# State sums two tiles at a time, and convolution taps loaded again for each image

## The chip, the cores and the metric

The kernel runs on one core of a Trainium2 chip. The metric is device time in microseconds (us), the median of several runs; lower is better. The core has five engines with a queue each: TensorE (PE) multiplies matrices into PSUM, VectorE (DVE) and GpSimd (POOL) work element by element, ScalarE (ACT) applies functions, and SyncE (SP) here issues nearly all DMAs. Each engine runs its own instructions in program order and waits on semaphores for the others.

## The reference, cut to what matters

The input `x` has four images of 128 channels and 64 x 64 pixels (L = 4096), in float32. Four layers follow, each of the form x + f(group_norm(x)):

```
x = x + attention(gn(x))        # one head over 4096 positions, 128 channels
x = x + conv5x5(gn(x))          # taps built from small tables by index
x = x + selective_scan(gn(x))   # 1x1 conv, two directions of 64 channels, 64 states each, 1x1 conv
x = x + conv3x3(gn(x))          # the offset branch of the reference does not change its result
```

The scan is the long part. For each channel and state it computes h[t] = exp(delta[t] * A) * h[t-1] + delta[t] * x[t] * B[t] over the 4096 positions, and then y[t] = sum over the 64 states of C[t] * h[t], plus D * x[t].

## The kernel before, in words

**The scan** (`scan_core`, L1159 to 1327) works in ticks. A tick is one tile of 128 partitions x 1024 positions: 32 channels of one direction with 4 states each. The loops run, outermost first, over image b, chunk c of 1024 positions, direction d, state group q (16 groups of 4 states), and channel group g (2 groups of 32): 256 ticks an image, 1024 in all. In each tick

- POOL makes the drive, `db = dx * br` (`drive`, L1227);
- ACT makes the decays, `da = exp(de * a)`, in two halves in PSUM, from three banks (`decay`, L1220);
- DVE scans them (`recur`, L1237) and multiplies the states by the row of C, into a tile `hc` (L1240); for two of five ticks or so POOL does this product instead (`weigh`, L1258);
- TensorE sums `hc` over states with a 128 x 32 matrix of ones, `sel`, into a PSUM bank `y` (`collect`, L1272). `collect` acts at every second tick, when both channel groups of a state group are there: 2 halves x 2 channel groups = 4 matmul instructions, each in 32 columns of the array, and each seen in the profile as two MATMULs. After the 16th state group a product with `skip` (L1283) closes the bank and ACT copies it out (`ys`, L1298).

The tiles `hc` come from a pool of 6. DMAs on SP's queue bring the operands four ticks ahead (`load`, L1188 to 1207): rows of B and C (`br`, `cr`, L1203) for each state group, `de` and `dx` (L1197) for each new chunk, direction and channel group.

**Everything else** is written as a generator, `images` (L1449), that yields an estimate of TensorE time after each few instructions. The loop at L1517 alternates between the scan's half ticks and this generator by a credit of 2.8 us a tick (`PACE`; 1.5 for the last image). So the instruction order on every engine is written out by this loop: while image b is scanned, attention, 5x5 convolution and operands of image b + 1 are woven between its ticks; the 3x3 convolutions of images 0 to 2 are woven into the scan of the last image, and the last one follows it (`conv_last`, L707).

**Attention** (`attention`, L434) takes score blocks of 128 x 512: a product `sc` (L479), an exponential on ACT into a ring of 8 slots (L485), and a product `acc` with the values (L491). The ring is the tile `exchange`, 128 x 4096, which later holds `delta` for the scan's operands. Every fourth block the sums of the exponentials are made on TensorE, in 32 columns as well (`sums`, L513). `sums_due` (L499) places them right after a `collect` where it can, by the mark "collected", and lets them wait three blocks at most.

**The 5x5 convolution** (`conv_pairs`, L810) treats output rows in pairs. Its matrices are the 25 taps and 10 sums of taps, all in one tile `cw` of 35 x 128 columns that stays in SBUF (L223). A chunk makes first `pq`, with the sums (`SUM12`, `SUM34`), and then two banks `pe`, with taps (L936). The first image uses four extra matrices in `more` and the pool `fill`, as nothing is scanned yet. The tables are built once on DVE (`build_conv_weights`, L231); 15 matrices are stored to DRAM in `kept` for a second program, which runs only if a sum of exponentials leaves its range. The first 15 places of `cw` serve the 3x3 convolution later.

Of the kernel before, what the change touches and what calls it, by code (L numbers as in the profile page):

```python
# [24 lines left out]
F32 = mybir.dt.float32  # L25
I32 = mybir.dt.int32
AF = mybir.ActivationFunctionType
ALU = mybir.AluOpType
# [4 lines left out]
P = 128  # L33
GROUPS = 32
GN_EPS = 1e-5
CH = 1024
# [16 lines left out]
def conv_preact_kernel(  # L53
# [166 lines left out]


    SUM12, SUM34, HSUM, HDIF = 5, 6, 7, 8
    cw = const.tile([P, NTAP + 10, C], F32, name="cw")  # L223
    taps5 = cw[:, :NTAP, :]

    m3 = cw[:, : main_w.shape[1], :]

    LSUM, LDIF, NKEPT = 9, 12, 15
    kept = dram.tile([P, NKEPT, C], F32, tag="kept", bufs=1, name="kept")

    def build_conv_weights(tmp):  # L231
        xx_sb = tmp.tile([P, NTAP, C], F32, name="xx_sb")
        nc.sync.dma_start(xx_sb, xhat)
        id_sb = tmp.tile([P, C], F32, name="id_sb")
        nc.sync.dma_start(id_sb, identity)
        picked = tmp.tile([P, 2, NTAP, C // 2], F32, name="picked")
        for n, (which, table, inds) in enumerate((("xx", wxx, indsxx), ("id", wid, indsid))):
            nr, oc = table.shape[1], table.shape[2]
            acc = picked[:, n]
            one = cw.rearrange("p k c -> p (k c)")[:, : NTAP * oc]  # L240
            one = one.rearrange("p (k o) -> p k o", o=oc)
            tab = tmp.tile([P, nr, oc], F32, name=f"tab{which}")
            nc.sync.dma_start(tab, table)
            ii = tmp.tile([P, NTAP], I32, name=f"ii{which}")
            nc.sync.dma_start(ii, inds.to_broadcast([P, NTAP]))
            fi = tmp.tile([P, NTAP], F32, name=f"fi{which}")
            nc.vector.tensor_copy(fi, ii)

            ng = tmp.tile([P, NTAP], F32, name=f"ng{which}")
            nc.vector.tensor_scalar(ng, fi, 0.0, float(nr), ALU.is_lt, ALU.mult)  # L250
            nc.vector.tensor_tensor(fi, fi, ng, ALU.add)
            nc.vector.tensor_scalar(fi, fi, 0.0, float(nr - 1), ALU.max, ALU.min)
            for r in range(nr):
                hit = tmp.tile([P, NTAP], F32, name=f"hit{which}{r}")
                nc.vector.tensor_scalar(hit, fi, float(r), None, ALU.is_equal)
                hit_b = hit.unsqueeze(2).to_broadcast([P, NTAP, oc])
                tab_b = tab[:, r : r + 1, :].to_broadcast([P, NTAP, oc])
                if r == 0:
                    nc.vector.tensor_tensor(acc, tab_b, hit_b, ALU.mult)
                else:  # L260
                    nc.vector.tensor_tensor(one, tab_b, hit_b, ALU.mult)
                    nc.vector.tensor_tensor(acc, acc, one, ALU.add)
                yield HOP

        for t in range(2):
            def every(ap):
                return ap.rearrange("p k (o t) -> p k o t", t=2)[:, :NTAP, :, t]

            idb = id_sb.rearrange("p (o t) -> p o t", t=2)[:, :, t].unsqueeze(1)
            idb = idb.to_broadcast([P, NTAP, C // 2])  # L270
            nc.vector.tensor_tensor(every(xx_sb), every(xx_sb), picked[:, 0], ALU.mult)
            nc.vector.tensor_tensor(every(cw), picked[:, 1], idb, ALU.mult)
            yield HOP
        nc.vector.tensor_tensor(taps5, taps5, xx_sb, ALU.add)
        for n in range(2):
            row = cw[:, (1 + 2 * n) * 5 :]
            nc.vector.tensor_tensor(
                cw[:, NTAP + n * 5 : NTAP + (n + 1) * 5, :], row[:, :5], row[:, 5:10], ALU.add
            )
        nc.sync.dma_start(kept, cw[:, :NKEPT, :])  # L280

# [150 lines left out]
    def attention(b, xs, xn, v, st, safe, loads):  # L434
# [188 lines left out]
        for w in (N - 2, N - 1) if fill else ():  # L623
            side_sums(w)
        blk = NM - 1
        values(N - 4)
        yield PRODUCT
        while due:
            sums(due.pop(0)[0])
            yield PRODUCT  # L630
        if not fill:
            sums(N - 1)
            yield PRODUCT
        evict_sums(blk)
        values(N - 3)
        yield PRODUCT
        turn(blk)
        values(N - 2)
        yield PRODUCT
        invert(blk)  # L640
        values(N - 1)
# [56 lines left out]


    def last_weights():  # L700
        half, above = cw[:, LSUM : LSUM + 3, :], cw[:, LDIF : LDIF + 3, :]
        nc.vector.tensor_tensor(half, m3[:, 0:3, :], m3[:, 6:9, :], ALU.add)
        nc.vector.tensor_scalar(half, half, 0.5, None, ALU.mult)
        nc.vector.scalar_tensor_tensor(above, m3[:, 3:6, :], -0.5, half, ALU.mult, ALU.add)
        nc.vector.scalar_tensor_tensor(half, m3[:, 3:6, :], 0.5, half, ALU.mult, ALU.add)

    def conv_last(b, xs, st, finish):  # L707
# [8 lines left out]
        def flat(t):  # L716
            return t.rearrange("p (h w) -> p h w", w=W)
# [30 lines left out]
        def products(acc, view, w):  # L748

            for n, dx in enumerate((1, 0, 2)):  # L750
                to = slice(max(1 - dx, 0), W - max(dx - 1, 0))
                of_ = slice(max(dx - 1, 0), W - max(1 - dx, 0))
                nc.tensor.matmul(  # L753
                    flat(acc)[:, :, to], cw[:, w + dx, :], view[:, :, of_],
                    start=n == 0, stop=n == 2, skip_group_check=True,
                )

# [36 lines left out]

    def more_weights(to):

        w = [cw[:, n * 5 : (n + 1) * 5, :] for n in range(3)]
        half, dif = to[:, 0], to[:, 1]  # L800
        nc.vector.tensor_tensor(half, w[0], w[2], ALU.add)
        yield HOP
        nc.vector.tensor_scalar(half, half, 0.5, None, ALU.mult)
        yield HOP
        nc.vector.scalar_tensor_tensor(dif, w[1], -0.5, half, ALU.mult, ALU.add)
        yield HOP
        nc.vector.scalar_tensor_tensor(half, w[1], 0.5, half, ALU.mult, ALU.add)
        yield HOP

    def conv_pairs(b, xs, tag, st, st2, lean):  # L810
# [87 lines left out]
        differences(0)  # L898
        K5 = 5
        steps, done = [], None  # L900

        def add(c, y, acc):
            i = 2 * c + y
# [6 lines left out]
        for c in range(L // CH):  # L910
# [20 lines left out]
            for n, (acc, parts) in enumerate(accs):  # L931
                k, total = 0, len(parts) * K5
                for w, view, r in parts:
                    for dx in range(K5):
                        k += 1
                        nc.tensor.matmul(  # L936
                            flat(acc), cw[:, w * K5 + dx, :] if w < HSUM else more[:, w - HSUM, dx, :],
                            view(r, dx), start=k == 1, stop=k == total and (n == 0 or not lean),
                        )
                        if k == 3 and done is not None:  # L940
                            done()
                            done = None
                        if k % 3 == 0:
                            yield 3 * PRODUCT
# [214 lines left out]
    def scan_core(mats4, ynds, before, widen, result):  # L1159
# [100 lines left out]
        def collect(i):  # L1260
# [2 lines left out]
            b, c, d, q, g = ticks[i]  # L1263
            if g + 1 < KG:
                return
            if q == 0:
                yacc[0] = bank("y", f"y_{b}_{c}_{d}")
            y = yacc[0]
            for h in range(CH // MM):
                for gg in range(KG):  # L1270
                    r = h * HALF + gg * SG
                    nc.tensor.matmul(  # L1272
                        y[r : r + SG, :], sel, hcs[i - KG + 1 + gg][:, bass.ts(h, MM)],
                        start=q == 0, stop=False, tile_position=(0, r), skip_group_check=True,
                    )
            ready.add("collected")
            for gg in range(KG):
                del hcs[i - KG + 1 + gg]
            if q + 1 < NQ:
                return  # L1280
            for h in range(CH // MM):
# [62 lines left out]
    def program(safe):  # L1344
# [2 lines left out]
        ready.clear()  # L1347
        shared.clear()
        if safe:
            nc.sync.dma_start(cw[:, :NKEPT, :], kept)  # L1350

        def load(tile, b):
            for c in range(NCH):
# [109 lines left out]
        with ExitStack() as es, tc.manual_schedule():  # L1463
# [19 lines left out]
            if not safe:  # L1483
                with tc.tile_pool(name="fill", bufs=2) as pools["fill"]:
                    while not (0, "begun") in ready:
                        next(work)
                    more = pools["fill"].tile([P, 2, 5, C], F32, tag="more", bufs=1, name="more")

                    with tc.tile_pool(name="tables", bufs=1) as tmp:
                        for _ in chain(scan_constants(), build_conv_weights(tmp), more_weights(more)):  # L1490
                            for _ in range(4):
                                next(work)
                    while (0, "convolved") not in ready:
                        next(work)
                del pools["fill"]
                setup.close()
            pools["rep"] = es.enter_context(tc.tile_pool(name=f"rep{safe}", bufs=3))
            pools["rows"] = es.enter_context(tc.tile_pool(name=f"rows{safe}", bufs=3))
            pools["hc"] = es.enter_context(tc.tile_pool(name=f"hc{safe}", bufs=6))
            pace = PACE  # L1500

            def before(b):
# [105 lines left out]
```

## Time and profile before

| | us |
|---|---|
| median of 3 runs | 4472.4 (4471.19 to 4475.15) |
| the profiled execution, its own time | 4469.3 |
| its span | 4467.5 |
| PE busy | 3980.8 (89%) |
| DVE busy | 3726.3 (83%) |
| POOL busy | 3638.1 (81%) |
| ACT busy | 2399.7 (54%) |
| `collect` on PE (L1272), 4096 MATMULs | 654.6 |
| DMA | 719.86 MB, 161 GB/s over the span |

A line of the profile names the source line, engine, operation, and output <- inputs by the program's tile names. "128*32" after a TensorE operation is the part of the array that it uses. Busy time of TensorE is modelled, as its instructions are pipelined: a MATMUL shows as about 0.6 us while the next one starts 0.43 us after it. PEld are weight loads. SPq is SP's queue of DMAs. The mean granted TensorE clock was 0.942 of full speed.

Stages by the span's time: image 0 without a scan to about 700 us; then attention, 5x5 convolution and operands of image 1 (738 to 1686), image 2 (1686 to 2633) and image 3 (2633 to 3540), each under the scan of the image before it; then the last scan to 4412, and the last 3x3 convolution to the end.

### The profile page before, as it was taken

To read this page: it belongs to the slowest core of one execution; us is meant where nothing else is said; L and a number is where in the kernel's file an instruction comes from. 1 tells how busy PE (TensorE), PEld (TensorE's weight loads), DVE (VectorE), ACT (ScalarE), POOL (GpSimd) and SP (SyncE) were. 2 spreads that over 40 slices of the span, in tenths; PEclk is the share of its full clock that TensorE was granted. 3 is DMA by queue.
4 is the path that set the end of the run, shared out by engine and by line. 5 is a ranking of instruction groups with operands and counts; after the bars stand their busy time and mean duration, and the time that the engine had idled before them with its cause. 6 is when DMAs were issued, how large, how long until landed. Compare 5 with 4: busy or idle time off the path is not lost. (4 is left out here: it accounts for less than half of the span.)

```text
span 4467.5 us, 43584 instructions
## 1 busy us (share of the span) xinstructions
PE 3980.8 (89%) x13480; PEld 1470.8 (33%) x13480; DVE 3726.3 (83%) x3703; ACT 2399.7 (54%) x4425; POOL 3638.1 (81%) x1728
## 2 busy tenths in 40 slices
PE   8999997999999979999999989999999758576776
PEld 4444433333333323333333333333333112121222
DVE  4712217999999989999999899999999899999995
ACT  3333217666665476666664576666654744444542
POOL 3433207999999978999999889999999889999995
PEclk9999999999999999999999999999999879787888
DMA  1000016544454565454545565455445666656562
GB/s 63 9 1 1 0 51 227 177 171 169 171 186 158 176 224 202 172 177 172 175 152 171 202 236 177 163 177 179 170 163 177 220 221 204 227 202 230 185 229 79
DMA packets 210002, 719.86 MB, mean 161 GB/s; under 512 B 24800, under 2 KB 25696, under 8 KB 209632
## 3 DMA queue, kind: packets, MB, share of 16 engines
q1 hardware_dynamic: 208160, 716.26, 45.9%
q8 instruction: 108, 1.77, 0.2%
q14 instruction: 134, 1.10, 0.1%
q10 hardware_dynamic: 1600, 0.73, 0.1%
HBM read 649.07 MB, written 67.83 MB: 160 GB/s over the span
## 5 line engine op out<-in xcount | busy, mean ns | idle before, releaser
L1227 POOL TENSOR_TENSOR db<-dx,br 128x1024 f32<-128x1024 f32 x1024 | 2399.9, 2365 | 231.1 <-DMA br<-bm 55.0
L1220 ACT ACTIVATE da<-de,a_neg 128x512 f32<-128x512 f32 (+1 forms) x1796 | 1342.9, 751 | 665.3 <-DVE da L1237 378.0
L479 PE MATMUL sc<-r,x 128*128 128x512 f32 x2048 | 1084.4, 612 | 16.0 <-ACT r L448 11.5
L491 PE MATMUL acc<-exchange,v 128*128 128x512 f32 x2048 | 1048.4, 594 | 1.7
L1258 POOL TENSOR_TENSOR hc<-hc,cr 128x1024 f32<-128x1024 f32 x401 | 947.7, 2363 | 19.3 <-ACT last L1253 16.5
L485 ACT ACTIVATE exchange<-sc 128x512 f32<-128x512 f32 x1024 | 604.7, 591 | 590.5 <-PE sc L479 583.8
L1272 PE MATMUL y<-hc,sel 128*32 128x512 f32 x4096 | 654.6, 652 | 270.6 <-POOL hc L1258 261.1
L1240 DVE TENSOR_TENSOR hc<-da,cr 128x512 f32<-128x512 f32 (+1 forms) x1078 | 835.5, 775 | 69.7 <-issue 0.9
L1237 DVE TENSOR_TENSOR_SCAN da<-da,last,db 128x512 f32<-128x512 f32 (+1 forms) x464 | 728.2, 1569 | 14.4 <-POOL db L1227 10.7
L1237 DVE TENSOR_TENSOR_SCAN da<-da,da,db 128x512 f32<-128x512 f32 x455 | 585.7, 1287 | 22.6 <-ACT da L1220 21.8
L479 PEld LDWEIGHTS sc<-r,x 128*128 128x128 f32 x2048 | 360.1, 190 | 607.8 <-issue 380.4
L491 PEld LDWEIGHTS acc<-exchange,v 128*128 128x128 f32 x2048 | 387.0, 190 | 496.7 <-issue 478.4
L1237 DVE TENSOR_TENSOR_SCAN hc<-da,last,db 128x512 f32<-128x512 f32 (+1 forms) x304 | 455.7, 1499 | 3.7 <-POOL db L1227 1.9
L1237 DVE TENSOR_TENSOR_SCAN hc<-da,hc,db 128x512 f32<-128x512 f32 x317 | 406.7, 1283 | 41.4 <-ACT da L1220 11.4
L533 POOL TENSOR_TENSOR sidep<-sidep,exchange 128x512 f32<-128x512 f32 x120 | 170.5, 1421 | 279.1 <-ACT exchange L485 276.9
L1272 PEld LDWEIGHTS y<-hc,sel 128*32 128x32 f32 x4096 | 92.9, 111 | 727.6 <-POOL hc L1258 350.9
L533 DVE TENSOR_TENSOR sided<-sided,exchange 128x512 f32<-128x512 f32 x120 | 96.1, 801 | 227.4 <-ACT exchange L485 226.1
L936 PE MATMUL pe<-df,cw 128*128 128x512 f32 x560 | 253.3, 597 | 0.0
L1237 DVE TENSOR_TENSOR_SCAN da<-da,db 128x512 f32<-128x512 f32 (+1 forms) x159 | 236.0, 1484 | 13.0 <-ACT da L1220 8.6
L678 PE MATMUL pcm<-xpm,cw 128*128 128x512 f32 x432 | 227.0, 670 | 15.5 <-ACT xpm L384 15.5
L513 PE MATMUL zp<-exchange,ones 128*32 128x512 f32 x1536 | 201.6, 596 | 8.0 <-DVE xs L580 7.9
L1253 ACT COPY last<-da 128x1 f32<-128x1 f32 x474 | 73.9, 156 | 249.4 <-DVE hc L1240 247.4
(239 smaller groups left out, 2829.8 us busy)
## 6 DMA issues: line engine op xcount, KB each, us to landing
br<-bm SPq DMA_DIRECT2D x512, 512.0 KB, 5.2
cr<-cm SPq DMA_DIRECT2D x512, 512.0 KB, 3.9
de<-dd SPq DMA_DIRECT2D x64, 512.0 KB, 4.7
dx<-dxd SPq DMA_DIRECT2D x64, 512.0 KB, 6.2
x<-in_x_dram SPq DMA_DIRECT2D x16, 512.0 KB, 5.1
xs<-in_x_dram SPq DMA_DIRECT2D x16, 512.0 KB, 5.6
xsd<-xs SPq DMA_DIRECT2D x16, 512.0 KB, 6.7
xcd<-xc SPq DMA_DIRECT2D x16, 512.0 KB, 2.8
```

What stands on the lines that cost most here:

```text
L479: nc.tensor.matmul(sc, xn[:, bass.ts(j, P)], rq[blk], start=True, stop=True)
L485: nc.scalar.activation(pt, sc, AF.Exp)
L491: nc.tensor.matmul(acc[blk], v[:, j, :], ring[:, u % NRING, :], start=j == 0, stop=j == NJT - 1)
L533: eng.tensor_tensor(s, s, ring[:, u % NRING, :], ALU.add)
L678: nc.tensor.matmul(acc.rearrange("p (r w) -> p r w", w=W), weights[:, t, :], xp[:, y : y + RPM, dx : dx + W], start=t == 0, stop=t == k * ...
L936: nc.tensor.matmul(flat(acc), cw[:, w * K5 + dx, :] if w < HSUM else more[:, w - HSUM, dx, :], view(r, dx), start=k == 1, stop=k == total ...
L1220: nc.scalar.activation(da, rep["de", b, c, d, g][:, bass.ts(h, size)], AF.Exp, scale=a_neg[:, at(i)])
L1227: nc.gpsimd.tensor_tensor(dbs[i], rep["dx", b, c, d, g], rows["b", b, c, d, q], ALU.mult)
L1237: nc.vector.tensor_tensor_scan(h, da, db[:, cut], before, ALU.mult, ALU.add)
L1240: nc.vector.tensor_tensor(hc[:, cut], h, rows["c", b, c, d, q][:, cut], ALU.mult)
L1258: nc.gpsimd.tensor_tensor(hcs[i], hcs[i], rows["c", b, c, d, q], ALU.mult)
L1272: nc.tensor.matmul(y[r : r + SG, :], sel, hcs[i - KG + 1 + gg][:, bass.ts(h, MM)], start=q == 0, stop=False, tile_position=(0, r), skip_gr ...
```

## The change

`collect` acts at every fourth tick: it sums two state groups in one go, 8 matmul instructions, the older group first. The last two groups of the last chunk are still summed one by one. The pool of `hc` grows from 6 to 8 tiles of 4 KB a partition.

To make room, `cw` (35 matrices) becomes `cs` (15): the ten sums of taps stay, and its places later hold the 3x3 weights. The 25 taps are built in the pool `fill`, used from there for image 0, and stored to DRAM with the sums. For images 1 to 3 they are loaded into the ring of exponentials at the end of each attention, slot by slot as the last products are issued: seven DMAs on SP (six of 512 columns, one of 128). `conv_pairs` takes its matrices from the ring, from `cs`, or from `more`. Nothing else is computed differently.

```diff
-    cw = const.tile([P, NTAP + 10, C], F32, name="cw")
-    taps5 = cw[:, :NTAP, :]
-    m3 = cw[:, : main_w.shape[1], :]
+    cs = const.tile([P, 15, C], F32, name="cs")
+    m3 = cs[:, : main_w.shape[1], :]
+    kept = dram.tile([P, NTAP, C], F32, tag="kept", bufs=1, name="kept")
+    kept_sums = dram.tile([P, 10, C], F32, tag="kept_s", bufs=1, name="kept_sums")
...
-        nc.sync.dma_start(kept, cw[:, :NKEPT, :])
+        nc.sync.dma_start(kept, cw)
+        nc.sync.dma_start(kept_sums, cs[:, :10, :])
...
+        def taps_to(n):
+            k = MM // C
+            to = ring[:, n, :].rearrange("p (k c) -> p k c", c=C)
+            part = kept[:, n * k : min((n + 1) * k, NTAP), :]
+            if not fill and part.shape[1]:
+                nc.sync.dma_start(to[:, : part.shape[1], :], part)
         values(N - 4)
         yield PRODUCT
         while due:
             sums(due.pop(0)[0])
             yield PRODUCT
+        for n in range(NRING - 4):
+            taps_to(n)
         if not fill:
             sums(N - 1)
             yield PRODUCT
+        taps_to(NRING - 4)
         evict_sums(blk)
         values(N - 3)
+        taps_to(NRING - 3)
         yield PRODUCT
         turn(blk)
         values(N - 2)
+        taps_to(NRING - 2)
         yield PRODUCT
...
+        taps5 = more[0] if wide else exchange(b)[:, : NTAP * C].rearrange("p (k c) -> p k c", c=C)
+        def matrix(w, dx):
+            if w < SUM12:
+                return taps5[:, w * K5 + dx, :]
+            if w < HSUM:
+                return cs[:, (w - SUM12) * K5 + dx, :]
+            return more[1][:, w - HSUM, dx, :]
...
-            if q == 0:
+            single = (b, c, d) == (B - 1, NCH - 1, 1) and q >= NQ - 2
+            if q % 2 == 0 and not single:
+                return
+            if q < 2:
                 yacc[0] = bank("y", f"y_{b}_{c}_{d}")
             y = yacc[0]
-            for h in range(CH // MM):
+            for back in range(0 if single else 1, -1, -1):
+                first = i - back * KG - KG + 1
+                for h in range(CH // MM):
+                    for gg in range(KG):
+                        r = h * HALF + gg * SG
+                        nc.tensor.matmul(
+                            y[r : r + SG, :], sel, hcs[first + gg][:, bass.ts(h, MM)],
+                            start=q == back, stop=False, tile_position=(0, r), skip_group_check=True,
+                        )
                 for gg in range(KG):
-                    r = h * HALF + gg * SG
-                    nc.tensor.matmul(
-                        y[r : r + SG, :], sel, hcs[i - KG + 1 + gg][:, bass.ts(h, MM)],
-                        start=q == 0, stop=False, tile_position=(0, r), skip_group_check=True,
-                    )
+                    del hcs[first + gg]
             ready.add("collected")
...
-            pools["hc"] = es.enter_context(tc.tile_pool(name=f"hc{safe}", bufs=6))
+            pools["hc"] = es.enter_context(tc.tile_pool(name=f"hc{safe}", bufs=8))
```

More of the change, by code (lines that the diff above doesn't have):

```diff
@@ L222, in conv_preact_kernel, with build_conv_weights @@
     SUM12, SUM34, HSUM, HDIF = 5, 6, 7, 8
-    cw = const.tile([P, NTAP + 10, C], F32, name="cw")
-    taps5 = cw[:, :NTAP, :]
-    m3 = cw[:, : main_w.shape[1], :]
-    LSUM, LDIF, NKEPT = 9, 12, 15
-    kept = dram.tile([P, NKEPT, C], F32, tag="kept", bufs=1, name="kept")
-    def build_conv_weights(tmp):
+    LSUM, LDIF = 9, 12
+    cs = const.tile([P, 15, C], F32, name="cs")
+    m3 = cs[:, : main_w.shape[1], :]
+    kept = dram.tile([P, NTAP, C], F32, tag="kept", bufs=1, name="kept")
+    kept_sums = dram.tile([P, 10, C], F32, tag="kept_s", bufs=1, name="kept_sums")
+    def build_conv_weights(tmp, cw):
+        taps5 = cw
         xx_sb = tmp.tile([P, NTAP, C], F32, name="xx_sb")
@@ L277, in build_conv_weights @@
             nc.vector.tensor_tensor(
-                cw[:, NTAP + n * 5 : NTAP + (n + 1) * 5, :], row[:, :5], row[:, 5:10], ALU.add
+                cs[:, n * 5 : (n + 1) * 5, :], row[:, :5], row[:, 5:10], ALU.add
             )
-        nc.sync.dma_start(kept, cw[:, :NKEPT, :])
+        nc.sync.dma_start(kept, cw)
+        nc.sync.dma_start(kept_sums, cs[:, :10, :])
     ASIZE, VSIZE = HP * (W + PAD) + PAD, (H + 2) * (W + 2) + PAD
@@ L700, in last_weights @@
     def last_weights():
-        half, above = cw[:, LSUM : LSUM + 3, :], cw[:, LDIF : LDIF + 3, :]
+        half, above = cs[:, LSUM : LSUM + 3, :], cs[:, LDIF : LDIF + 3, :]
         nc.vector.tensor_tensor(half, m3[:, 0:3, :], m3[:, 6:9, :], ALU.add)
@@ L753, in products @@
                 nc.tensor.matmul(
-                    flat(acc)[:, :, to], cw[:, w + dx, :], view[:, :, of_],
+                    flat(acc)[:, :, to], cs[:, w + dx, :], view[:, :, of_],
                     start=n == 0, stop=n == 2, skip_group_check=True,
@@ L786, in conv_last, with more_weights @@
             yield HOP
-    def more_weights(to):
+    def more_weights(cw, to):
         w = [cw[:, n * 5 : (n + 1) * 5, :] for n in range(3)]
@@ L936, in conv_pairs @@
                         nc.tensor.matmul(
-                            flat(acc), cw[:, w * K5 + dx, :] if w < HSUM else more[:, w - HSUM, dx, :],
-                            view(r, dx), start=k == 1, stop=k == total and (n == 0 or not lean),
+                            flat(acc), matrix(w, dx), view(r, dx),
+                            start=k == 1, stop=k == total and (n == 0 or not lean),
                         )
@@ L1265, in collect @@
                 return
-            if q == 0:
+            single = (b, c, d) == (B - 1, NCH - 1, 1) and q >= NQ - 2
+            if q % 2 == 0 and not single:
+                return
+            if q < 2:
                 yacc[0] = bank("y", f"y_{b}_{c}_{d}")
             y = yacc[0]
-            for h in range(CH // MM):
-                for gg in range(KG):
-                    r = h * HALF + gg * SG
-                    nc.tensor.matmul(
-                        y[r : r + SG, :], sel, hcs[i - KG + 1 + gg][:, bass.ts(h, MM)],
-                        start=q == 0, stop=False, tile_position=(0, r), skip_group_check=True,
-                    )
+            for back in range(0 if single else 1, -1, -1):
[7 more added lines that the diff above has]
+                        )
+                for gg in range(KG):
+                    del hcs[first + gg]
             ready.add("collected")
-            for gg in range(KG):
-                del hcs[i - KG + 1 + gg]
             if q + 1 < NQ:
@@ L1349, in program @@
         if safe:
-            nc.sync.dma_start(cw[:, :NKEPT, :], kept)
+            nc.sync.dma_start(cs[:, :10, :], kept_sums)
         def load(tile, b):
@@ L1486, in program @@
                         next(work)
-                    more = pools["fill"].tile([P, 2, 5, C], F32, tag="more", bufs=1, name="more")
+                    more = [
+                        pools["fill"].tile([P, NTAP, C], F32, tag="taps", bufs=1, name="taps"),
+                        pools["fill"].tile([P, 2, 5, C], F32, tag="more", bufs=1, name="more"),
+                    ]
                     with tc.tile_pool(name="tables", bufs=1) as tmp:
-                        for _ in chain(scan_constants(), build_conv_weights(tmp), more_weights(more)):
+                        for _ in chain(scan_constants(), build_conv_weights(tmp, more[0]), more_weights(*more)):
                             for _ in range(4):
```

## The prediction

> **What bounds the kernel now.** I read the page's slices first, to see whether one engine sets the pace throughout.
>
> ```profile
> PE   8999997999999979999999989999999758576776
> DVE  4712217999999989999999899999999899999995
> POOL 3433207999999978999999889999999889999995
> PEclk9999999999999999999999999999999879787888
> ```
>
> Each digit is a fortieth of the span, 112 us. From slice 7 to 31 three engines are near full together; in the last quarter TensorE (PE) falls behind while DVE and POOL stay full. So the question is asked by stage. I cut the span where TensorE's products change: attention of image 1 (738 to 1391 us), its 5x5 convolution (to 1580), its operands (to 1686), the same for images 2 and 3, then the last scan (from 3540). Three such rows, busy us by engine (image 2, and the last scan):
>
> ```profile
> core 0: us, PE busy (x) PEld busy (x) DVE busy (x) ACT busy (x) POOL busy (x), PEclk, DMA share, GB/s
> ...
> 1686.00:2335.00 649.00, 639.35 (x2434) 234.85 (x2434) 611.53 (x631) 413.88 (x855) 600.91 (x261) 1.00 0.51 175
> 2335.00:2525.00 190.00, 182.63 (x560) 66.82 (x560) 178.65 (x196) 85.55 (x135) 178.60 (x84) 0.97 0.49 169
> ...
> 3540.00:4412.00 872.00, 578.91 (x1700) 158.20 (x1700) 829.50 (x508) 409.02 (x653) 811.62 (x371) 0.79 0.59 210
> ```
>
> TensorE is at 98.5% of the attention stage, DVE at 94%, POOL at 93%. In the convolution it is at 96%, the other two at 94%, and the missing 4% is one idle of about 8 us at its start. In the last scan TensorE is at 66% and cannot be the bound. Busy matmuls are modelled, so I checked the starts of TensorE's instructions in the timeline of the attention stage (start, duration, merged count):
>
> ```profile
> 2000.39 1.07 PE L1272 MATMUL y<-hc,sel 128*32 128x512 f32 x8
> 2001.28 1.04 PE L513 MATMUL zp<-exchange,ones 128*32 128x512 f32 x8
> 2002.25 1.12 PE L479 MATMUL sc<-r,x 128*128 128x512 f32 x2
> 2003.21 1.02 PE L491 MATMUL acc<-exchange,v 128*128 128x512 f32 x2
> 2004.07 1.02 PE L479 MATMUL sc<-r,x 128*128 128x512 f32 x2
> 2004.93 1.02 PE L491 MATMUL acc<-exchange,v 128*128 128x512 f32 x2
> 2005.88 1.07 PE L1272 MATMUL y<-hc,sel 128*32 128x512 f32 x8
> 2006.88 1.13 PE L479 MATMUL sc<-r,x 128*128 128x512 f32 x2
> 2007.84 1.02 PE L491 MATMUL acc<-exchange,v 128*128 128x512 f32 x2
> ```
>
> From start to start a full-width product costs 0.86 us (2003.21 to 2004.07) and the stream has no hole. The one just before a state sum costs 0.95 (2004.93 to 2005.88), the sum itself 1.00 (to 2006.88), the product just after it 0.96 (to 2007.84). A sum followed by another 32-column group, the exponentials' (L513), costs 0.89 (2000.39 to 2001.28). So going into narrow columns costs 0.09, coming out 0.11 in the sum and 0.10 after it: 0.30 us for each visit.
>
> Who else is close to waiting: the waits of DVE and of the scalar engine in the same window (total us, times, longest).
>
> ```profile
> DVE da L1237 <- ACT da L1220: 11.2, 15, 2.9
> ...
> ACT exchange L485 <- PE sc L479: 110.1, 116, 2.5
> ACT da L1220 <- DVE da L1237: 49.7, 53, 2.7
> ...
> SPq L1203 <- POOL hc L1258: 270.7, 66, 10.1
> ```
>
> DVE loses about 16 of 649 us to waits, mostly for decays, and the rest of its 37 idle us lies in small gaps between instructions, so it is about 97% used. ACT is tied to both neighbours in program order: it waits for scores and for decay banks. TensorE and DVE are two near-equal bounds joined by ACT.
>
> **What the Trainium skill says.** "TensorEngine Tiling (Array Packing)", Key Properties: "Mode switching requires drain". The trace agrees, with the 0.30 us above. "TensorE: Matmul & The Clock Gate", Part 3, The mechanism: matmuls start and end in program order, without reordering; so a longer sum holds up the scores behind it, and the timeline shows none overtaking. "DMA: Bandwidth & Descriptors", Anatomy of one DMA — SWDGE (gpsimd) path: a semaphore wait happens on the issuing sequencer before dispatch; so a tap load that waits for TensorE holds every load behind it on SP, as SP's 270.7 us before L1203 show.
>
> **The change, part by part.** The sum is made against the profiled execution's 4469.3 us (span 4467.5); the median of the runs is 4472.4, 3.1 higher, and I add that at the end.
>
> *State sums in pairs (L1260 to 1278).* The 2048 matmul instructions stay; only their place moves. Two lone visits cost 2 x (0.09 + 1.00 + 0.10) = 2.38 us, a merged one 0.09 + 0.89 + 1.00 + 0.10 = 2.08. But a sum was often neighbour to an L513 group and shared its visit, because `sums_due` waits for a sum to stand beside, and now there are half as many. So not every pair gains. I counted the steps from other work into 32-column work in TensorE's instruction order of both kernels: 506 become 349. By stage: attention 311 to 246 (65 fewer), convolution 80 to 40 (40 fewer), operands 9 fewer, last scan and its back ends 43 fewer. The last 43 are worth nothing: TensorE waits there, 257.3 us in the last scan for L1258's products alone. The 9 in the operand stages fall where TensorE is 75% busy; nothing too.
>
> Attention: 65 x 0.30 = 19.5 us of TensorE's time; convolution: 40 x 0.30 = 12.0. TensorE gains 1% in attention, 2% in convolution, but DVE has only about 3% left and is coupled to it. I take 55% in attention, my estimate for two near-equal stations in a row: 10.7 us; and half in the convolution, where POOL has 4% left: 6.0. Ends: none (0) to all (31.5).
>
> *The longer visit.* A sum holds TensorE 1.88 us instead of 1.00, every four ticks instead of two (a tick is one 128 x 1024 state tile, some 3.5 us). Queued behind it are the scores, behind those ACT's exponentials, and behind these in ACT's queue the next tick's decay that DVE needs. What hides the extra 0.88 us is DVE's three decay banks (L1218), 1.5 ticks or 5 us of work. In the 55% I have already put a small loss; if the cover were gone, see the last rival.
>
> *Two more buffers (hc 6 to 8).* A state tile waits up to two ticks longer for its sum, so the two buffers only restore the old distance: the scan of tick 4k+8 needs the sum issued at 4k+6, as 2k+6 needed 2k+4. No DVE wait on TensorE for hc is in the profile. Cost and gain 0.
>
> *Taps reloaded.* Seven DMAs for each of three images: 6 of 256 KB and one of 64 KB, 1.6 MB. When the first four are issued, the products that read their slots are already queued; the others follow TensorE's last products. In the stage 175 GB/s take 0.51 of the DMA engines, so about 168 GB/s are free: 1.6 MB take some 10 us. Image 1's last attention product starts at 1383.6 and the first product with a tap (`pe`) at 1410.35, 26 us later, since the ten `pq` products use only sums that stay in SBUF. The load is hidden. What it can cost is on SP: six issues at 0.6 us each, as the queue's rows for `dx` show, and a wait for TensorE, ahead of the loads of decays and drives for the next chunk (`de`, `dx`), which POOL already waits for (13.3 us in this window). Bound: 0 to 8 us an image. POOL has 7% to spare, so I take 1 us each, 3 in all.
>
> *Moved weights, larger store.* 2240 KB instead of 960 KB go to DRAM at 185 us; SP's next work comes at 639 us, which hides it. Matmuls from `cs`, `taps` or `exchange` have the shapes they had. 0.
>
> Sum: 4469.3 - 10.7 - 6.0 + 3.0 = 4455.6; with the 3.1, **4459**.
>
> **The rivals.** *TensorE alone is the bound*: all 31.5 us come through, the operands' 9 x 0.30 = 2.7 too, the loads cost nothing: 4472.4 - 34.2 = 4438. For it: the hole-free stream. Against it: DVE's 97%.
>
> *The gain goes into other waits*: DVE and POOL keep the pace, TensorE waits longer elsewhere, the taps cost 3: 4475. For it: ACT's 50 us of waits for DVE's banks. Against it: TensorE's own waits in the stage come to 7 us.
>
> *Slower*: the long visit stalls DVE. There are 138 doubled sums in attention and 40 in convolution, 178. If a third of the 0.88 us, 0.29, is not made good, that is 52 us against 31.5, plus 3: 4496. It decides from (31.5 + 9 - 3) / 178 = 0.21 us a sum. For it: ACT already waits 116 times for a score, up to 2.5 us, and also for the sum that ends a chunk (L1298). Against it: DVE then waits only 15 times in 649 us.
>
> That the change does not do what it says I can exclude for the order of sums; the 157 fewer visits are in it.
>
> **How the numbers follow.** The forecast's own case, 4448 to 4463: 45%. TensorE alone, 4432 to 4448: 20%. Gain eaten, 4464 to 4481: 21%. Slower: 14%. A difference under 0.2%, 9 us, is about what a measurement of this kernel cannot tell from none. So faster 65%, same 21%, slower 14%. The range 4436 to 4484 leaves out the end of the first rival and most of the last.
>
> **What would show it.** Right: lone sums of 16 matmuls at some 1.9 us, attention stages 3 to 5 us shorter each, convolutions 2, the last scan unchanged; DVE at 95% in attention; SP's tap loads landing before 1400 us. Wrong: attention as long as before with more waits of DVE for decays or of TensorE for exponentials; POOL held for `dx` by more than 5 us just after each tap load; a change in the last scan, where I have none.

## The result, and the profile after

The changed kernel takes 4459.63 us (median of 7 runs, 4456.99 to 4461.58); the kernel before, run on the same chip beside it, 4471.47 (7 runs, 4468.12 to 4475.15). The ratio is 0.9972, interval 0.9962 to 0.9983: a gain of 0.28%, about 12 us, where 13 were forecast. The profiled execution took 4459.63 us, its span 4457.8. So the total was met; most of this section is about why its parts were not.

The page's slices of the changed kernel, to be set against those of before:

```profile
PE   8999997999999979999999889999999657575666
DVE  3712217999999979999999889999999899999995
POOL 3433207999999978999999889999999889999995
PEclk9999999999999989999999989999999768787888
```

TensorE (PE) has lost a tenth in a few slices of the last quarter, where it is not the bound; DVE and POOL are as full as before. The stages (same windows as in the prediction: attention, convolution, last scan):

```profile
core 0: us, PE busy (x) PEld busy (x) DVE busy (x) ACT busy (x) POOL busy (x), PEclk, DMA share, GB/s
...
1686.00:2335.00 649.00, 631.24 (x2429) 235.98 (x2427) 610.85 (x642) 412.62 (x851) 599.05 (x264) 0.99 0.50 176
2335.00:2525.00 190.00, 179.56 (x568) 69.59 (x568) 178.87 (x198) 85.32 (x137) 179.46 (x85) 0.97 0.50 172
...
3540.00:4412.00 872.00, 547.06 (x1695) 160.21 (x1695) 829.15 (x504) 403.90 (x642) 813.55 (x373) 0.77 0.59 206
```

In attention TensorE is busy 8.1 us less in the same 649 us, but DVE 0.7 less and POOL 1.9 less: they have hardly moved forward. The sums themselves are as forecast. TensorE's timeline in the attention stage, below the line of dots around a lone merged sum, above it at another place that will matter:

```profile
1962.76 1.02 PE L449 MATMUL pr<-x,wqk 128*128 128x512 f32 x2
1965.42 1.13 PE L482 MATMUL sc<-r,x 128*128 128x512 f32 x2 [1.65 <-ACT last L1278]
...
2023.00 1.93 PE L1303 MATMUL y<-hc,sel 128*32 128x512 f32 x16
2024.86 1.12 PE L482 MATMUL sc<-r,x 128*128 128x512 f32 x2
2025.82 1.02 PE L494 MATMUL acc<-exchange,v 128*128 128x512 f32 x2
```

Sixteen MATMULs in one visit take 1.86 us from start to start (2023.00 to 2024.86), and the product after them 0.96: the 0.89 + 1.00 and 0.10 of the prediction. The 1.93 beside it is the modelled end. The Trainium skill says this of TensorE's records too ("Perfetto Trace Analysis", Tensor Engine Instruction (MATMUL, LD_WEIGHTS): the end is estimated, not observed), which is why starts are read here. At 1962.76 the stream now has a hole: 2.66 us between two starts, 1.65 of them a wait for ACT (ScalarE).

Waits of ACT, DVE and TensorE in the same attention stage (total us, times, longest); the last line below is one of the kernel before that the prediction did not show:

```profile
ACT exchange L488 <- PE sc L482: 79.9, 89, 3.2
ACT da L1245 <- DVE da L1262: 72.1, 64, 2.1
...
DVE da L1262 <- ACT da L1245: 8.7, 9, 2.7
DVE hc L1262 <- ACT da L1245: 5.1, 9, 1.0
...
PE sc L482 <- ACT last L1278: 3.0, 3, 1.6
...
DVE hc L1237 <- ACT da L1220: 2.5, 9, 0.6
```

ACT waits less for scores than before (110.1 us then) and more for DVE to give a decay bank back (49.7 then). DVE itself waits no more for decays: 13.8 us in its two lines, 13.7 before (11.2 and 2.5). The work has slid from waiting for TensorE to waiting for DVE; this is what a second bound looks like.

For the account I cut both traces at events, since fixed windows hide a shift: attention from its first to its last `acc` product, convolution to its last `pe`, operands to the next first `acc`. Sums over images 1 to 3 (us):

| | before | after | measured | forecast |
|---|---|---|---|---|
| start, to image 1's first `acc` | 742.8 | 739.8 | -2.9 | 0 |
| attention (3) | 1919.0 | 1916.7 | -2.3 | -10.7 |
| convolution (3) | 573.7 | 559.6 | -14.1 | -6.0, and loads +3.0 |
| operands (2) | 230.5 | 237.8 | +7.3 | 0 |
| rest, last scan and end | 1001.4 | 1003.9 | +2.4 | 0 |
| span | 4467.5 | 4457.8 | -9.7 | -13.7 |

Single executions drift by some us in places (a kernel below has a trace 5.6 us longer at an equal median), so the small rows say little alone. Five pairs of kernels that differ by the pairing, this one and four from the experiments, give this range: start -0.3 to -4.6, attention -0.5 to -8.3, convolution -9.7 to -14.1, operands +1.4 to +7.6, rest with a mean of +0.6. Convolution and operands belong together, as part of what TensorE gains there is waited out before the next image: of the 7.3 us by which the two operand stages grew in this pair, 5.9 are idle time of TensorE (59.4 to 65.3), mostly for ACT's `xn`, and 1.4 busy time. Its granted clock there fell too, from 0.87 to 0.81 and 0.83; as matmuls made slower would show as busy time, that accounts for 1.4 us at most. Together the two rows have a mean of -5.8 over the five pairs. In attention the clock was 1.00 in both kernels.

Attention needs the closer look. TensorE's time without its waits (waits counted from starts, so good to some tenths) went from 631.9, 630.0, 630.5 us (images 1 to 3) to 625.2, 625.4, 624.8: 17.0 less in all, for 63 visits fewer in the trace. But its waits went from 26.5 to 41.3, 14.8 more. Nearly half of that is at the query points. Once per 32 score blocks TensorE makes the next query block (`pr`, L449) in PSUM bank `s`, of which there is one, ACT copies it to `r`, and the next score needs that bank again. Of the 21 such points in three images 10 were open before, costing 9.2 us; now 15 are, costing 16.3. All ten of before show 0.78 us of idle in the profile, and so do twelve of the 15; three show 1.49 to 1.67, the one at 1962.76 among them. There ACT came late, as its own timeline shows:

```profile
1963.59 0.69 ACT L1245 ACTIVATE da<-de,a_neg 128x512 f32<-128x512 f32 x1 [1.42 <-DVE da L1262]
...
1964.69 0.68 ACT L451 ACTIVATE r<-pr,bqk 128x512 f32<-128x512 f32 x1
```

It stood 1.42 us until DVE gave a decay bank back, and the copy to `r` was queued behind. So of the 7.1 us of growth some 4.6 are five more open points at 0.92, and some 2.5 are ACT held by DVE. TensorE's timeline of the kernel before shows a covered point and an open one:

```profile
1888.19 1.02 PE L446 MATMUL pr<-x,wqk 128*128 128x512 f32 x2
1889.14 1.07 PE L1272 MATMUL y<-hc,sel 128*32 128x512 f32 x8
1890.99 1.13 PE L479 MATMUL sc<-r,x 128*128 128x512 f32 x2
...
1968.73 1.02 PE L446 MATMUL pr<-x,wqk 128*128 128x512 f32 x2
1970.53 1.12 PE L479 MATMUL sc<-r,x 128*128 128x512 f32 x2 [0.78 <-ACT last L1253]
```

(Between 1889.14 and 1890.99 stands an L513 group.) At 1889.14 a state sum happens to stand between query and score and hides ACT's copy. State sums were every second tick and are now every fourth, so they stand there half as often: 11 points covered by 32-column work before, 6 after. That could be counted in the instruction order beforehand. The other waits that grew are those of `zp` groups for DVE's eviction of their bank, 9.8 to 13.0 us, and of scores for exponentials that stand behind decays in ACT's queue, about 1.0 to 4.2.

So two theories for the 8 us that attention fell short by: **lost cover** (a merged sum is missing where it hid a wait) and **DVE's coupling** (what TensorE saves is soon DVE's). The rivals: the loads and POOL were tested as well; the longer visit is judged from the traces alone.

### The profile page after: what moved, and what is told of

It reads as the page before. It is cut to its first block, busy times and chain, and to the rows that moved or that the text cites. A ratio compares the mean times of both kernels' runs of the same rounds, so it can differ in the third digit from the quotient of the medians.

```text
span 4457.8 us, 43613 instructions
## 1 busy us (share of the span) xinstructions
PE 3917.5 (88%) x13480; PEld 1490.3 (33%) x13480; DVE 3722.1 (83%) x3703; ACT 2397.3 (54%) x4425; POOL 3638.0 (82%) x1728
## 5 line engine op out<-in xcount | busy, mean ns | idle before, releaser
L1303 PE MATMUL y<-hc,sel 128*32 128x512 f32 x4096 | 601.8, 645 | 266.3 <-POOL hc L1283 253.4
L1262 DVE TENSOR_TENSOR_SCAN da<-da,last,db 128x512 f32<-128x512 f32 (+1 forms) x464 | 728.1, 1569 | 15.3 <-POOL db L1252 13.1
L1303 PEld LDWEIGHTS y<-hc,sel 128*32 128x32 f32 x4096 | 114.2, 112 | 692.1 <-POOL hc L1283 341.8
L695 PE MATMUL pcm<-xpm,cs 128*128 128x512 f32 x432 | 213.8, 644 | 34.4 <-ACT xpm L387 34.4
L961 PE MATMUL pe<-df,exchange 128*128 128x512 f32 x480 | 213.7, 595 | 0.0
```

Source lines behind the costliest of these rows:

```text
L695: nc.tensor.matmul(acc.rearrange("p (r w) -> p r w", w=W), weights[:, t, :], xp[:, y : y + RPM, dx : dx + W], start=t == 0, stop=t == k * ...
L961: nc.tensor.matmul(flat(acc), matrix(w, dx), view(r, dx), start=k == 1, stop=k == total and (n == 0 or not lean),)
L1262: nc.vector.tensor_tensor_scan(h, da, db[:, cut], before, ALU.mult, ALU.add)
L1303: nc.tensor.matmul(y[r : r + SG, :], sel, hcs[first + gg][:, bass.ts(h, MM)], start=q == back, stop=False, tile_position=(0, r), skip_grou ...
```

## The experiments

All times are medians; ratios are to the kernel before on the same chip, with a 95% interval.

### The loads and the buffers alone

`reload_hc6` is the changed kernel with every sum made alone, as before, and 6 buffers: of the change only the tap loads, moved weights and larger store remain. `reload_hc8` is the same with 8 buffers.

```diff
-            single = (b, c, d) == (B - 1, NCH - 1, 1) and q >= NQ - 2
+            single = True
...
-            if q < 2:
+            if q == 0:
...
-            pools["hc"] = es.enter_context(tc.tile_pool(name=f"hc{safe}", bufs=8))
+            pools["hc"] = es.enter_context(tc.tile_pool(name=f"hc{safe}", bufs=6))
```

(The last two lines are in `reload_hc6` alone.)

> The weights' half of the change alone: taps in the ring, sums in cs, state sums two groups of channels at a time as before, hc with 6 buffers. If the loads are hidden: the time of before, ratio 1.000, within 2 us. If the loads hold SP's other loads up, as the prediction priced them: 3 us or more above before. If the earlier start of the scan (drive of tick 48 is 3 us earlier in the changed kernel) comes from the weights' place: 3 us below before.

> The same with hc of 8 buffers. If spare buffers are worth nothing, as predicted: equal to the run with 6 buffers within 2 us. If they let DVE and POOL run ahead where the scan starts: 3 to 4 us below it, all before tick 48, and that much of the change's 12 us is not due to the sums.

Measured: 4471.81 us (13 runs), ratio 1.000 (0.9992 to 1.0008), and 4470.48, ratio 0.9997 (0.9989 to 1.0005). Neither the loads' cost nor a gain by the buffers shows: the medians are 0.4 and 1.8 us below the kernel before, the attention stages within 0.5 and the convolutions within 0.6. The gain comes with the pairing. (The intervals, some 3.6 us to each side, would by themselves admit the 3 us forecast for the loads.) In the changed kernel the loads land as the page's list of DMA issues says (KB each, median us from issue to landing):

```profile
exchange<-kept SPq DMA_DIRECT2D x18, 256.0 KB, 4.3
...
exchange<-kept SPq DMA_DIRECT2D x3, 64.0 KB, 5.1
```

For image 1 six issues start at 1374.47 us and take 2.96 us of SP together, the seventh goes out at 1380.14, and the first product with a tap starts at 1405.3. Landing in at most 5.8 us, they are early by more than 15 us. POOL's waits for `dx`, the sign that the prediction named for loads held up, did not grow (53.4 us in the whole span before, 49.4 after). The 1 us an image in the forecast was a guess between 0 and 8; nothing of it was seen.

### The merged sum split again

`split_visit` puts between the two halves of a merged sum a product of full width that adds zeros to one column of `y`, so the narrow mode is left and entered again. Buffers, order and loads stay.

```diff
+    none = const.tile([P, 1], F32, name="none")
+    nc.gpsimd.memset(none, 0.0)
...
+                if back:
+                    nc.tensor.matmul(
+                        y[:, 0:1], ident, none, start=False, stop=False, skip_group_check=True
+                    )
```

> The changed kernel with one full-width product of a zero column (into the same bank, nothing is added to it) between the two halves of each paired sum, so that every pair makes two visits to the narrow columns again. If the gain is the visits' time where TensorE is the bound, it goes back by 0.3 to 0.4 us a pair there: with all 178 pairs of attention and convolution some 60 us of TensorE time; in the convolution alone 40 pairs, some 12 to 15 us. If attention is held by DVE as much as by TensorE: attention longer by only a part, the total 4470 to 4485. If the gain comes from summing later and less often and not from the visits: 4460, as the changed kernel.

Measured: 4516.97 us, ratio 1.010 (1.0085 to 1.0116), 57 us above the changed kernel: attention +44.7, convolution +15.3. Its TensorE timeline, and below the line of dots one of the kernel before:

```profile
2005.85 1.07 PE L1305 MATMUL y<-hc,sel 128*32 128x512 f32 x8
2006.84 0.38 PE L1312 MATMUL y<-none,ident 128*128 128x1 f32 x2
2007.16 1.06 PE L1305 MATMUL y<-hc,sel 128*32 128x512 f32 x8
2008.15 1.13 PE L484 MATMUL sc<-r,x 128*128 128x512 f32 x2
...
2012.01 0.95 PE L556 MATMUL pz<-zsel,zs 128*128 128x1 f32 x8
2012.82 1.10 PE L479 MATMUL sc<-r,x 128*128 128x512 f32 x2
```

From the first half's start to the score are 2.30 us, where the merged sum takes 1.86: the detour costs 0.44 us. Not all of it is the two changes of mode: `pz`, also of full width and one column, among full-width products, takes 0.81 us for eight MATMULs, so the two of the detour would cost about 0.20 by themselves (an estimate from these two lines). That leaves about 0.24 for the changes of mode. (That a change of mode drains the array is what the page cited in the prediction states.) TensorE's time without waits rises by 19.6 us in each attention stage, and the stages grow by 14.2, 14.2 and 16.2. So of 58.8 us *added* to TensorE 44.7 arrived, and some 14 filled waits, which fell from 41.3 us to about 27. Of the 17.0 us *removed* 2.3 arrived, and 14.8 had become waits. In both directions the waits of TensorE took up some 14 us, growing in the one case and shrinking in the other; that added time counts for more than removed time is not shown, as the two amounts differ so much. The case of the expectation in which TensorE is the bound came true (some 60 us); its middle, 4470 to 4485, took DVE as equal to TensorE and was missed. TensorE is still the first bound, with little room below it.

### DVE relieved

In both kernels DVE makes no product with C at every fifth tick, and the unweighted states are summed. This leaves out part of the computation, to free DVE.

```diff
-                h = hc[:, cut] if to_pool(i) else da
+                h = hc[:, cut] if to_pool(i) or i % 5 == 0 else da
...
-                if not to_pool(i):
+                if not to_pool(i) and i % 5:
```

> The kernel before with DVE relieved: every fifth tick, where DVE would multiply the states by C, the product is left out (the states are summed as they are), 1.4 us of DVE in 5 ticks, 8% of its work. If DVE shares the bound in attention: attention stages shorter only as far as TensorE lets them, 5 to 10 us each; the last scan, bound by DVE and POOL, 30 us or so; in all 4410 to 4440. If TensorE alone holds attention: attention unchanged.

> The changed kernel with the same product left out. If DVE is what kept the visits' 19.5 us in attention from showing, they show now: 20 to 30 us below the relieved kernel before, of which attention 4 to 7 us a stage. If the longer visit gives the time back in attention whatever DVE does: 10 to 14 us below, as in the full kernels, attention stages the same within 1 us.

Measured: 4440.06 us, ratio 0.9926 (0.9912 to 0.9939), and 4421.25, ratio 0.9883 (0.9868 to 0.9898). The pairing is now worth 18.8 us by the medians, against 11.8 with DVE full. The intervals are too wide to call that difference settled; the stages speak more clearly. Attention shrinks by 8.3 us through the pairing instead of 2.3, out of 16.4 removed from TensorE. And relieving DVE alone shortens the attention stages of the kernel before by 14.2 us, though TensorE has no less to do: DVE did hold TensorE up. (The last scan was expected to gain 30 us or so from this; the part from the last convolution on gained 8.) Waits of DVE in the attention window of the changed kernel, relieved:

```profile
DVE hc L1262 <- ACT da L1245: 27.6, 39, 2.3
DVE da L1262 <- ACT da L1245: 24.8, 21, 2.9
```

52 us instead of 14, so here DVE follows the others, and still half of what TensorE lost in work came back as waits: 15.1 us of them before, 22.9 after. The query points show both causes apart: with DVE relieved again 10 of 21 are open before and 15 after, but all of them show 0.78 us of idle; the three long ones are gone. DVE's coupling is real and does not explain everything.

### POOL relieved

One in five of POOL's products with C is left out (321 instead of 401), and the states are summed unweighted.

```diff
-            if to_pool(i):
+            if to_pool(i) and i % 10 != 1:
```

> The kernel before with POOL relieved instead: in every tenth tick, where POOL would multiply the states by C, the product is left out, 2.4 us of POOL in 10 ticks, 7% of its work. If POOL does not hold attention: attention stages unchanged within 2 us; the last scan somewhat shorter.

> The changed kernel with POOL relieved. If DVE and not POOL is the second bound in attention: 10 to 16 us below the relieved kernel before, attention the same within 1 us a stage, and only the convolutions gain a little more. If POOL is: 20 to 30 us below, with attention 4 to 7 us shorter a stage.

Measured: 4465.1 us, ratio 0.9985 (0.9978 to 0.9991), and 4455.32, ratio 0.9962 (0.9948 to 0.9975). Pairing 9.8 us, attention -0.5. In the attention window of the changed kernel POOL's busy time fell from 599 to 557 us, while the three stages together got 1.6 us shorter (3.4 in the kernel before), and the three long query points are still there. POOL is not what holds attention.

### Products moved from DVE to POOL

POOL makes the products with C of three ticks in seven instead of two in five, only where attention and convolution run (420 products instead of 401); nothing is left out.

```diff
-                    else n % 2 == 0 if "operands" in ready else n % 2 == 1
+                    else n % 2 == 0 if "operands" in ready else i % 7 % 2 == 1
```

> The changed kernel with work moved from DVE to POOL in attention and convolution: POOL multiplies the states by C in three ticks of seven instead of two of five (outside the operand stages and the last image). DVE loses 0.04 us a tick, POOL gains 0.07. If DVE held attention and POOL had room: 2 to 4 us shorter for each attention stage, 4448 to 4455. If POOL is as near its limit as DVE: 4458 to 4466, with the convolutions longer.

> The same move in the kernel before, where TensorE still needs 5 to 7 us more in each attention stage: less to gain, 4468 to 4473. If it gains as much here as in the changed kernel, DVE is the bound in both and the sums' pairing has little to do with it.

Measured: 4456.63 us, ratio 0.9966 (0.9952 to 0.998), and 4462.7, ratio 0.9977 (0.9967 to 0.9988). In the changed kernel DVE goes to about 93.6% in attention, POOL to 95.0%, and attention does not change (1917.2 us; 1919.9 in the kernel before). What DVE gives, POOL seems to take up; so small a move shows nothing. The changed kernel fell between the two ranges expected, and the kernel before missed its own: it gains 9 us at the median, more than the changed one (3), so that the pairing is worth 6.1 us by these medians. Why, I leave open: the trace of the kernel before, of an execution of 4469.1 us, doesn't show it.

### The query points covered

One value product, otherwise issued just after the score behind a query, goes before it (L597 to 606). TensorE then has 0.86 us of work while ACT copies. It is the same work in another order.

```diff
+            w = u - 2
+            early = j == 18 and blk + 1 < NM
+            if early:
+                values(w)
             scores(u)
             cost += PRODUCT
-            w = u - 2
             if w >= 0:
                 if w < N - HELD:
-                    values(w)
+                    if not early:
+                        values(w)
```

> The changed kernel with one value product put ahead of the score that follows the next block's queries, so that TensorE does not wait 0.9 us for ACT there, seven times an attention: 6 us of TensorE's time a stage. If DVE is the bound in attention since the change: 0 to 2 us a stage, 4454 to 4460, and other waits of TensorE grow by the rest. If TensorE is: 5 us a stage, 4442 to 4448.

> The kernel before with the value product ahead of the score that follows the queries. There 10 of the 21 query points under a scan leave TensorE waiting 0.92 us for ACT, against 15 in the changed kernel, where fewer state sums stand at that place. If this lost cover is what ate the pairing's gain in attention, the edit is worth less here than the 17 us there: 4460 to 4466, and the pairing is then worth 18 to 24 us with the edit in both. If DVE's near bound ate it, the edit is worth as much here as there: 4453 to 4457, and the pairing stays at 12 us.

Measured: with the pairing 4442.16 us, ratio 0.9933 (0.992 to 0.9947), 17.5 below the changed kernel; without it 4457.08, ratio 0.9968 (0.9956 to 0.998), 14.5 below the kernel before. The hole is gone from TensorE's timeline here:

```profile
2034.70 1.02 PE L449 MATMUL pr<-x,wqk 128*128 128x512 f32 x2
2035.56 1.02 PE L494 MATMUL acc<-exchange,v 128*128 128x512 f32 x2
2036.50 1.99 PE L482 MATMUL sc<-r,x 128*128 128x512 f32 x4
```

0.94 us from the value product's start to the score's, no wait. Three of the 21 points keep a wait, of 0.54 to 0.82 us, where ACT comes late. TensorE's waits in the three attention stages fall from 41.3 to 29.0, the stages by 11.0 (1905.7), and image 1's attention starts 4.7 us earlier, as image 0's gains too. The kernel before gains less in attention, 5.5 (1913.5), having had fewer holes. So with a ready product at every query point in both, the pairing brings 7.8 us in attention instead of 2.3: 5.5 of what was missing are put down to lost cover. (These are single traces; in the kernel before and the two with loads alone, attention agrees within 0.5 us.) Over the whole it is worth 14.9 us by the medians, between the 18 to 24 of "lost cover alone" and the 12 of "cover has no part". Neither theory stands alone. (The interval on 14.9 would admit either end; the stages decide.)

The five pairs sort themselves the same way. Attention falls by 2.3, 0.5 and 2.7 us in the three that leave both causes in place (as it is, POOL relieved, products moved) and by 8.3 and 7.8 in the two that remove one. A pair with both removed was not tried.

### Both edits

`after_both` is the changed kernel with the value product early and the products moved.

> Both edits in the changed kernel. If two near-equal bounds hold attention, relieving both gives more than the sum of the two alone: 4436 to 4448, below every kernel so far. If one of them does nothing, it equals the other alone.

Measured: 4438.9 us, ratio 0.9926 (0.9912 to 0.9939). It is the fastest that computes everything, 0.74% under the kernel before and 20.7 us under the changed one. The two edits alone gave 3.0 and 17.5, so they add up; more than the sum, as expected of two near-equal bounds, was not seen. From `after_early` it differs by 3.3 us, with intervals that overlap.

## Why the prediction was right, point by point

**The total** was right, 4459.6 against 4459, but partly by errors that cancelled: attention gave some 4 us in the mean of the pairs instead of 10.7, the loads showed no cost instead of 3, and the start came out 2.7 us earlier in that mean, where I had nothing. For this last I have only an argument (fewer visits around the first ticks); the kernels with loads alone don't show it (+1.7, +2.5).

**The price of a visit**, 0.30 us, held: sums, stages (17.0 us for 63 visits is 0.27 each) and the split sum, at 0.44 for two changes of mode and a product of about 0.20, agree with it roughly.

**Attention, 55% of 19.5**: the step that failed. The share arriving was 2.3 of 17.0 in this pair and 4.3 in the mean of five. DVE's coupling was named; how much passes, 55%, was my estimate for two near-equal stations, and it was too much. What was not named at all is that a visit also hides waits: the count of the steps into 32-column work took each removed visit as a saving and did not ask what it stood in front of. So 14.8 of the 17.0 us saved came back as waits, 7.1 of them at the query points.

**Convolution, half of 12.0**: the size was right, -5.8 with the operands, but not the place. The convolution stages alone shrank by 11.6 in the mean, nearly all of the 12.0, and the operand stages, where the prediction had nothing, gave half of it back. That the operands' 9 visits cost nothing cannot be told apart in this sum.

**The longer visit** as a cause of slowness: no sign of it. DVE's waits for decays are 13.8 us in the window, 13.7 before. The three decay banks seem to have been cover enough; no run tested it alone.

**Buffers, moved weights, last scan** at 0: right. The lead over the kernel before is 9.4 us at tick 768, where the last scan begins, and 10.2 at its end, while TensorE shows 32 us less busy time in the window of the last scan.

**The signs to watch**: lone sums of 1.9 us and taps landed before 1400 us came; attention 3 to 5 us shorter each did not (it was 0.4 and 0.7 us longer, then 3.4 shorter), the convolutions shrank by 3.3 to 6.5 each instead of 2, and DVE did not rise to 95% (94.3, 94.4, 94.4% before, 94.7, 94.3, 94.6 after). More waits of TensorE in attention, a sign of "wrong", were there, though most were for copies and bank evictions and few for the exponentials that it named; more waits of DVE for decays or of POOL for `dx`, the other such signs, were not.

## What to carry to other kernels

Before an instruction is taken out of a full stream, look at what stands behind it: if the next one waits for another engine, the removed one was its cover, and the saving is that much less. The order of instructions shows this without a run, and filling the hole with a neighbour that is ready can be worth more than the change (17.5 us here against 12). Where two engines are near-equal and a third ties them in program order, a small saving on one can go almost wholly into waits (14.8 of 17.0 us here), and time added to it fills such waits first (some 14 of 58.8).

## What the runs showed of the hardware

Unexpected was how much of a change the waits take up: of 17.0 us removed from TensorE in attention 2.3 showed, of 58.8 added 44.7, so that some 14 us were lost to its waits or made up by them. And a 128 x 1 product of full width between two 32-column groups takes 0.32 us from start to start and lengthens the sum by 0.44, while one among full-width products takes about 0.20 (`pz`) and one with 512 columns 0.86. Loads of 1.6 MB beside a DMA share of about 0.50 left no mark on the time that could be measured (ratio 1.000, 0.9992 to 1.0008), in three places.
